# Second layer of a four-layer image network: one kept query projection and keys-first softmax attention without row maxima or transposes

## The chip, the cores and the metric

The kernel runs on one core of a Trainium2 chip. The metric is the device time of one execution in microseconds (us), as a median over runs. All runs that are compared in this document were fast: none was over 1.5% above the fastest of its kernel. A profile of one execution stands beside each kernel. Its engines are PE (TensorE matmuls), PEld (TensorE weight loads), DVE (VectorE), ACT (ScalarE), POOL (GpSimd) and SP (SyncE). PEclk is the share of full speed that TensorE's clock was granted.

## The reference

Four layers, each `x = x + layer(group_norm(x))`, run on two images of 512 channels and 64x64 pixels. The change concerns the second layer, an attention with 8 heads of 64 channels. Its 256 keys and values come from bilinear samples of the query image at places that the queries themselves choose:

```python
q = einsum('oc,bchw->bohw', w_q, x)
oi = q.reshape(b * g, inner // g, h, w)          # 8 offset groups
...                                              # offsets from every 4th pixel of oi
kv_feats = grid_sample_bilinear(oi, vgrid)       # 16 x 16 samples of q
k, v = split(einsum('oc,bchw->bohw', w_kv, kv_feats))
...
sim = einsum('bhid,bhjd->bhij', qh * 64 ** -0.5, kh)   # 4096 queries, 256 keys
out = einsum('bhij,bhjd->bhid', softmax(sim), vh)
return einsum('oc,bchw->bohw', w_out, out) + b_out
```

## The kernel before

Everything is float32. P = 128 partitions, C = 512 channels in KC = 4 chunks of 128 (two heads each), blocks of TB = 512 tokens (NB = 8 of them), NT = 4 token tiles in a block, NK = 256 keys. Two image buffers fill most of SBUF; the second (Y) lends its space to weights in this layer. The queries are projected twice: once with tokens on partitions for the sampling, and once per block for the attention.

```python
# sampling, for each of 32 token tiles t
for kc in range(KC):
    matmul(ps, X[:, kc, t * P:(t + 1) * P], wq[:, kc, :], ...)      # q, tokens first
vector.tensor_tensor(q, ps, row, ALU.add)
...                                       # wt = max(0,1-|dy|) max(0,1-|dx|), 128x2048
for g in range(NH):
    cc, lo = g // 2, (g % 2) * HD
    matmul(acc[lo:lo + HD, cc, :NK], q[:, g * HD:(g + 1) * HD], wt[:, g, :], ...)
# attention: for blk in range(NB), for cc in range(KC)
self.project(ps, wq[:, :, cc * P:(cc + 1) * P], X, blk)             # q again, channels first
scalar.activation(q, ps, AF.Identity, bias=bq[:, cc:cc + 1], scale=HD ** -0.5)
for h in range(2):
    self.scores(pS, q, keys[:, cc, :], h)        # tokens first: 4 matmuls of 256 columns
    vector.tensor_reduce(nm, pS, AX.X, ALU.max, negate=True)        # row maxima
    for t in range(NT):
        scalar.activation(prob[:, t, :], pS[:, t, :], AF.Exp, bias=nm[:, t:t + 1],
                          accum_out=sm[:, t:t + 1])
    vector.reciprocal(sm, sm)
    vector.tensor_tensor(prob, prob, bcast(sm, 2, NK), ALU.mult)
    self.weighted(psO, prob, vals[...], h, wp, pp)   # 8 transposes, 2 copies, 2 matmuls
scalar.copy(att[:, cc, :], psO)
# after the four chunks: self.add_projected(X, wo, att, blk, pp, bias)
```

## Time and profile before

| kernel before | value |
|---|---|
| time | 10124.43 us, median of 3 runs (10123.72 to 10126.53) |
| second layer, first image: sampling | 2259.6 to 2453.4 = 193.8 us |
| keys and values | to 2468.2 = 14.8 us |
| attention with output projection | to 3230.2 = 762 us |
| second image | the same stages about 5050 us later |

The page opens with the busy time of each engine, its share of the span and its number of instructions.

```profile
span 10124.4 us, 68201 instructions
PE 8632.9 (85%) x25390; PEld 4059.3 (40%) x25390; DVE 4276.9 (42%) x7503; ACT 2048.9 (20%) x4873; POOL 1093.5 (11%) x1190
```

Eighty-five per cent of PE says that PE matters, but not where there is slack; the prediction looks for that stage by stage.

### The profile page before, as it was taken

Reading aid. Unit: us, or ns where it says so; the run is one execution under the profiler, and the core shown is the slowest. Engines: PE = TensorE matmul, PEld = TensorE weight load, DVE = VectorE, ACT = ScalarE, POOL = GpSimd, SP = SyncE. Lnnn points to the kernel's source line nnn. Section 1 sums busy time; section 2 is a strip of 40 time slices with the busy share of each in tenths; the row PEclk is TensorE's granted clock in tenths of the full one; section 3 lists DMA queues with packets and bytes.
Section 4 is the critical chain, followed back from the end, with each engine's and each line's share of the span. In section 5 each row is a group of like instructions: output and inputs, shape, how many; then the busy total and the mean of one; then the engine's idle time right before and its main releaser. Section 6 shows DMA issues by size and latency. Waiting matters only on the chain. (4 is left out here: it accounts for less than half of the span.)

```text
span 10124.4 us, 68201 instructions
## 1 busy us (share of the span) xinstructions
PE 8632.9 (85%) x25390; PEld 4059.3 (40%) x25390; DVE 4276.9 (42%) x7503; ACT 2048.9 (20%) x4873; POOL 1093.5 (11%) x1190
## 2 busy tenths in 40 slices
PE   7989898988786699888889898989888876998887
PEld 3333333344333255544443333333443332555443
DVE  3444444425334922244434444444352359222343
ACT  1111111105222101222211111111142221022222
POOL 0222222200000000000002222222000000100000
PEclk9878888889887889977788887887898888899877
DMA  1000000000000000100000000000000000000000
GB/s 46 0 4 0 3 0 0 0 22 1 0 0 9 1 0 5 38 9 13 9 15 0 4 0 4 0 0 0 22 1 0 0 9 1 0 5 5 13 9 13
DMA packets 34324, 66.76 MB, mean 7 GB/s; under 512 B 2532, under 2 KB 15076, under 8 KB 32970
## 3 DMA queue, kind: packets, MB, share of 16 engines
q1 hardware_dynamic: 33994, 62.40, 1.8%
q8 instruction: 202, 3.31, 0.1%
q14 instruction: 128, 1.05, 0.0%
HBM read 45.62 MB, written 16.78 MB: 6 GB/s over the span
## 5 line engine op out<-in xcount | busy, mean ns | idle before, releaser
L122 PE MATMUL mm<-big,w 128*128 128x512 f32 x2560 | 1371.4, 682 | 0.0
L122 PEld LDWEIGHTS mm<-big,w 128*128 128x128 f32 x2560 | 532.6, 221 | 727.4 <-issue 639.9
L449 POOL TENSOR_TENSOR acc<-acc,prod 128x512 f32<-128x512 f32 x512 | 663.4, 1296 | 1441.3 <-DVE prod L444 1392.6
L442 PE MATMUL mm<-lt,taps 18*128 18x512 f32 x1152 | 761.2, 804 | 0.0
L166 PE MATMUL mm<-cst,prob 128*128 128x128 f32 x2048 | 429.7, 370 | 273.0 <-DVE prob L524 247.9
L388 PE MATMUL mm<-prod,cst 128*18 128x512 f32 x1152 | 648.5, 713 | 0.0
L169 DVE COPY pT<-mm 128x512 f32<-128x512 f32 x384 | 265.5, 691 | 787.4 <-PE mm L166 787.4
L166 PEld LDWEIGHTS mm<-cst,prob 128*128 128x128 f32 x2048 | 342.7, 194 | 511.3 <-issue 508.7
L154 PE MATMUL pS<-proj,big 64*128 64x256 f32 x2048 | 459.4, 444 | 98.5 <-ACT big L772 49.9
L444 DVE TENSOR_TENSOR prod<-vx,mm 128x512 f32<-128x512 f32 x512 | 351.9, 687 | 443.9 <-PE mm L442 356.6
L384 DVE TENSOR_TENSOR prod<-qs,kx 128x512 f32<-128x512 f32 x576 | 443.2, 800 | 195.6 <-PE mm L388 194.3
L713 PE MATMUL acc<-big,dg 128*128 128x512 f32 x768 | 369.0, 639 | 136.3 <-DVE big L681 71.4
L171 ACT COPY pT<-mm 128x512 f32<-128x512 f32 x384 | 224.8, 585 | 1000.8 <-PE mm L166 1000.8
L681 DVE TENSOR_TENSOR big<-big 128x3968 f32<-128x3968 f32 x96 | 410.4, 4286 | 21.2 <-PE acc L713 18.3
L442 PEld LDWEIGHTS mm<-lt,taps 18*128 18x128 f32 x1152 | 241.4, 232 | 424.9 <-issue 245.9
L154 PEld LDWEIGHTS pS<-proj,big 64*128 64x128 f32 x2048 | 307.1, 211 | 242.4 <-ACT big L772 103.7
L166 PE MATMUL mm<-cst,qf 128*128 128x128 f32 x1024 | 207.1, 354 | 219.0 <-DVE qf L884 219.0
L420 ACT ACTIVATE prob<-pS,nm 128x256 f32<-128x256 f32 x512 | 235.8, 473 | 630.9 <-DVE nm L415 625.7
L173 PE MATMUL psO<-pT,ctxm 128*64 128x512 f32 x512 | 334.2, 788 | 33.0 <-ACT pT L171 33.0
L173 PE MATMUL psO<-pT,vals 128*64 128x512 f32 x512 | 361.7, 800 | 0.0
L516 DVE TENSOR_REDUCE nm<-pS 128x4 f32<-128x1024 f32 x128 | 150.7, 1219 | 480.8 <-PE pS L154 480.8
L154 PE MATMUL pS<-proj,q 64*128 64x256 f32 x1024 | 280.2, 522 | 53.4 <-ACT q L863 53.4
(267 smaller groups left out, 11377.5 us busy)
## 6 DMA issues: line engine op xcount, KB each, us to landing
big<-in_x SPq DMA_DIRECT2D x8, 2048.0 KB, 8.3
out<-big SPq DMA_DIRECT2D x16, 1024.0 KB, 4.1
w<-in_W_kv SPq DMA_DIRECT2D x16, 256.0 KB, 3.8
big<-in_w_kv SPq DMA_DIRECT2D x2, 2048.0 KB, 7.8
w_sr<-in_W_sr SPq DMA_DIRECT2D x2, 1024.0 KB
w<-in_W_q SPq DMA_DIRECT2D x8, 256.0 KB, 3.0
w_proj<-in_W_proj SPq DMA_DIRECT2D x2, 1024.0 KB, 5.4
big<-in_w_out SPq DMA_DIRECT2D x2, 1024.0 KB
```

The source lines that it names most:

```text
L122: self.nc.tensor.matmul(ps, w[:, kc, :], X[:, kc, blk * TB:(blk + 1) * TB], start=(kc == 0), stop=(kc == KC - 1))
L154: self.nc.tensor.matmul(pS[:, t, :], q[lo:lo + HD, t * P:(t + 1) * P], keys[lo:lo + HD, :], start=True, stop=True)
L166: nc.tensor.transpose(ps[:, t * P:(t + 1) * P], prob[:, t, k2 * P:(k2 + 1) * P], self.ident)
L169: nc.vector.tensor_copy(pT, ps)
L173: nc.tensor.matmul(psO[h * HD:(h + 1) * HD, :], vals[:, k2, :], pTs[k2], start=(k2 == 0), stop=(k2 == 1))
L384: nc.vector.tensor_tensor(pr.rearrange("p (y x) -> p y x", x=W), qs.rearrange("p (y x) -> p y x", x=W), kx[:, dy:dy + 8, dx:dx + W], ALU.mult)
L388: nc.tensor.matmul(ps[:18, :], self.cst[:, C_TAP + 8 - k:C_TAP + 26 - k], pr, start=(k == 0), stop=(k == 8))
L442: nc.tensor.matmul(ps, taps[:, k, :], lt, start=True, stop=True)
L444: nc.vector.tensor_tensor(pr.rearrange("p (y x) -> p y x", x=W), vx[:, dy:dy + 8, dx:dx + W], ps.rearrange("p (y x) -> p y x", x=W), ALU.mult)
L449: nc.gpsimd.tensor_tensor(acc, acc, pr, ALU.add)
L681: nc.vector.tensor_tensor(o, a, b, ALU.max)
L713: nc.tensor.matmul(accs[b], dg, p2[:, b * TB:(b + 1) * TB], start=(j == 1), stop=(j == 6))
```

## The change

The intent is to project the queries once, keep them in the spare image buffer for the whole layer, and form the scores with keys on partitions. Exponentials of keys-first scores can go into the value product directly, so the transposes fall away. The sum over keys becomes a product with ones, and the division is done once on the small result. A row maximum is awkward in that form, so it is left out. A bound on |q| times |k| is computed instead; only if it exceeds 40 does the whole general program (the old code) run again at the end. For the given inputs the bound is under 9. The diff, cut to its core; the output projection of block b is now issued two steps late, and the scores of step i+1 are issued before the values of step i:

```diff
+        def query(blk):                                   # in sampling, a block ahead
+            for cc in range(KC):
+                self.project(ps, wq[:, :, cc * P:(cc + 1) * P], X, blk)
+                nc.scalar.activation(Y[:, cc, blk * TB:(blk + 1) * TB], ps, AF.Identity,
+                                     bias=bq[:, cc:cc + 1])
         for each token tile t:
-            4 matmuls of 512 columns (q, tokens first), DVE adds the row, DVE and 2 ACT passes for wt
+            nc.scalar.activation(wt, ycoord, AF.Abs, bias=yneg[:, t:t + 1])
+            nc.vector.tensor_scalar(wt, wt, -1.0, 0.0, ALU.add, ALU.min)
+            nc.vector.tensor_tensor(wt, wt, hatx, ALU.mult)
+            for cc in range(KC):
+                nc.tensor.transpose(ps[:, cc * P:(cc + 1) * P], Y[:, cc, t * P:(t + 1) * P], ident)
+            nc.scalar.copy(q, ps)
...
+    def product_bound(self, q, keys, sp, pp):             # after the values
+        nc.vector.tensor_reduce(top[:, :, 0], q, AX.X, ALU.max, apply_absolute_value=True)
+        nc.vector.tensor_reduce(top[:, :, 1], keys, AX.X, ALU.max, apply_absolute_value=True)
...
+    def exponentials(self, q, keys, wp, pp):
+        for j in range(2):                                # 128 keys each
+            pS = [pp.tile([P, TB], F32, name="mm") for _ in range(2)]
+            for h in range(2):
+                nc.tensor.matmul(pS[h], keys[h * HD:(h + 1) * HD, j * P:(j + 1) * P],
+                                 q[h * HD:(h + 1) * HD, :], start=True, stop=True)
+            for h in range(2):
+                nc.scalar.activation(prob[h][j], pS[h], AF.Exp)
+        for h in range(2):
+            nc.gpsimd.tensor_tensor(total[h], prob[h][0], prob[h][1], ALU.add)
+    def attended(self, out, made, vals, wp, ppo, ppd):
+        for j in range(2):
+            for h in range(2):
+                nc.tensor.matmul(psO[h * HD:(h + 1) * HD, :], vals[:, j, h * HD:(h + 1) * HD],
+                                 prob[h][j], start=(j == 0), stop=(j == 1))
+        for h in range(2):
+            nc.tensor.matmul(psD[h * HD:(h + 1) * HD, :], self.one[:, :HD], total[h], ...)
+        nc.vector.reciprocal(r, psD)
+        nc.vector.tensor_tensor(out, psO, r, ALU.mult)    # into Y, over the used queries
```

More of the change, by code (lines that the diff above doesn't have):

```diff
@@ L25 @@
 NK = 256
+LIMIT = 40.0
+RISKS = 16
 C_ID, C_GRP, C_MEAN, C_ONE, C_E2, C_TAP, C_Y, C_X, C_MH = (
@@ L50, in in_turn @@
         gens = [g for g in gens if next(g, gens) is not gens]
-class Net:
+class General:
+    risk = None
     def __init__(self, tc, cst, vec):
@@ L914, in softplus, with layer1, query_and_sample, at_most @@
         return out
+class Net(General):
+    def layer1(self, X, Y, d):
+        tc, nc, vec = self.tc, self.nc, self.vec
+        with tc.tile_pool(name="l1", bufs=1) as sp:
+            wq = sp.tile([P, KC, C], F32, name="wq1")
+            nc.sync.dma_start(wq, d["w_q1"].rearrange("(kc p) o -> p kc o", p=P))
+            wkv = sp.tile([P, KC, 2 * C], F32, name="wkv1")
+            nc.sync.dma_start(wkv, d["w_kv1"].rearrange("(kc p) o -> p kc o", p=P))
+            bq = sp.tile([P, KC], F32, name="bq1")
+            feats = sp.tile([P, KC, NK], F32, name="feats")
+            with tc.tile_pool(name="l1a", bufs=1) as wp, \
+                    tc.tile_pool(name="l1p", bufs=4, space=PSUM) as pp, \
+                    tc.tile_pool(name="l1k", bufs=1, space=PSUM) as ppk:
+                grid = wp.tile([P, 2, NK], F32, name="grid")
+                nc.sync.dma_start(grid, d["grid"])
+                nmean, rstd, _ = self.group_stats(X, sp, pp)
+                self.scale_rows(wq, rstd)
+                self.shift_bias(bq, wq, nmean, pp)
+                ycoord, hatx = self.sample_grid(X, wq, bq, grid, wp, pp)
+                self.query_and_sample(X, Y, wq, bq, ycoord, hatx, feats, wp, pp, ppk)
+            with tc.tile_pool(name="l1c", bufs=1) as late:
+                keys = late.tile([P, KC, NK], F32, name="keys")
+                vals = late.tile([P, 2, C], F32, name="vals")
+                with tc.tile_pool(name="l1q", bufs=4, space=PSUM) as pp:
+                    for oc in range(KC):
+                        ps = pp.tile([P, TB], F32, name="mm")
+                        for kc in range(KC):
+                            nc.tensor.matmul(ps[:, :NK], wkv[:, kc, oc * P:(oc + 1) * P],
+                                             feats[:, kc, :], start=(kc == 0), stop=(kc == KC - 1))
+                        nc.scalar.mul(keys[:, oc, :], ps[:, :NK], HD ** -0.5)
+                    for t in range(2):
+                        ps = pp.tile([P, TB], F32, name="mm")
+                        for kc in range(KC):
+                            nc.tensor.matmul(ps, feats[:, kc, t * P:(t + 1) * P], wkv[:, kc, C:],
+                                             start=(kc == 0), stop=(kc == KC - 1))
+                        nc.vector.tensor_copy(vals[:, t, :], ps)
+                    self.product_bound(Y, keys, sp, pp)
+                with tc.tile_pool(name="l1b", bufs=2) as wp, \
+                        tc.tile_pool(name="l1s", bufs=5, space=PSUM) as pp, \
+                        tc.tile_pool(name="l1o", bufs=2, space=PSUM) as ppo, \
+                        tc.tile_pool(name="l1d", bufs=1, space=PSUM) as ppd:
+                    wo = wp.tile([P, KC, C], F32, name="wo1", bufs=1)
+                    nc.sync.dma_start(wo, d["w_out1"].rearrange("(kc p) o -> p kc o", p=P))
+                    steps = [(blk, cc) for blk in range(NB) for cc in range(KC)]
+                    probs = {}
+                    for i in range(len(steps) + 2):
+                        if i < len(steps):
+                            blk, cc = steps[i]
+                            probs[i] = self.exponentials(Y[:, cc, blk * TB:(blk + 1) * TB],
+                                                         keys[:, cc, :], wp, pp)
+                        if 1 <= i <= len(steps):
+                            blk, cc = steps[i - 1]
+                            self.attended(Y[:, cc, blk * TB:(blk + 1) * TB], probs.pop(i - 1),
+                                          vals[:, :, cc * P:(cc + 1) * P], wp, ppo, ppd)
+                        if i >= 2 and steps[i - 2][1] == KC - 1:
+                            blk = steps[i - 2][0]
+                            self.add_projected(X, wo, Y[:, :, blk * TB:(blk + 1) * TB], blk, pp,
+                                               vec[:, V_BOUT:V_BOUT + KC])
+    def query_and_sample(self, X, Y, wq, bq, ycoord, hatx, feats, wp, pp, ppk):
+        nc = self.nc
+        acc = ppk.tile([P, KC, TB], F32, name="acc")
+        n_t = N // P
+        yneg = wp.tile([P, n_t], F32, name="yneg")
+        nc.vector.tensor_scalar(yneg, self.cst[:, C_Y:C_Y + n_t], -1.0, None, ALU.mult)
+        nc.vector.tensor_scalar(hatx, hatx, -1.0, None, ALU.mult)
+        def query(blk):
+            for cc in range(KC):
+                ps = pp.tile([P, TB], F32, name="mm")
+                self.project(ps, wq[:, :, cc * P:(cc + 1) * P], X, blk)
+                nc.scalar.activation(Y[:, cc, blk * TB:(blk + 1) * TB], ps, AF.Identity,
+                                     bias=bq[:, cc:cc + 1])
+        query(0)
+        for blk in range(NB):
+            if blk + 1 < NB:
+                query(blk + 1)
+            for t in range(blk * NT, (blk + 1) * NT):
+                wt = wp.tile([P, NH, NK], F32, name="wt", bufs=2)
+                nc.scalar.activation(wt, ycoord, AF.Abs, bias=yneg[:, t:t + 1])
+                nc.vector.tensor_scalar(wt, wt, -1.0, 0.0, ALU.add, ALU.min)
+                nc.vector.tensor_tensor(wt, wt, hatx, ALU.mult)
+                ps = pp.tile([P, TB], F32, name="mm")
+                for cc in range(KC):
+                    nc.tensor.transpose(ps[:, cc * P:(cc + 1) * P], Y[:, cc, t * P:(t + 1) * P],
+                                        self.ident)
+                q = wp.tile([P, C], F32, name="q_tok", bufs=2)
+                nc.scalar.copy(q, ps)
+                for g in range(NH):
+                    cc, lo = g // 2, (g % 2) * HD
+                    nc.tensor.matmul(acc[lo:lo + HD, cc, :NK], q[:, g * HD:(g + 1) * HD],
+                                     wt[:, g, :], start=(t == 0), stop=(t == n_t - 1))
+        nc.vector.tensor_copy(feats, acc[:, :, :NK])
+    def product_bound(self, q, keys, sp, pp):
+        nc = self.nc
+        top = sp.tile([P, KC, 2], F32, name="top_qk")
+        nc.vector.tensor_reduce(top[:, :, 0], q, AX.X, ALU.max, apply_absolute_value=True)
+        nc.vector.tensor_reduce(top[:, :, 1], keys, AX.X, ALU.max, apply_absolute_value=True)
+        nc.vector.tensor_tensor(top[:, :, 0], top[:, :, 0], top[:, :, 1], ALU.mult)
+        ps = pp.tile([P, TB], F32, name="mm")
+        nc.tensor.matmul(ps[:2, :KC], self.e2, top[:, :, 0], start=True, stop=True)
+        self.at_most(ps[:2, :KC])
+    def at_most(self, bounds):
+        nc = self.nc
+        n = bounds.shape[0]
+        nc.vector.tensor_reduce(self.risk[:n, self.risks:self.risks + 1], bounds, AX.X, ALU.max)
+        self.risks += 1
+    def exponentials(self, q, keys, wp, pp):
+        nc = self.nc
+        prob = [[wp.tile([P, TB], F32, name="prob", bufs=8) for _ in range(2)] for _ in range(2)]
+        for j in range(2):
[5 more added lines that the diff above has]
+                nc.scalar.activation(prob[h][j], pS[h], AF.Exp)
+        total = [wp.tile([P, TB], F32, name="total", bufs=4) for _ in range(2)]
+        for h in range(2):
+            nc.gpsimd.tensor_tensor(total[h], prob[h][0], prob[h][1], ALU.add)
+        return prob, total
+    def attended(self, out, made, vals, wp, ppo, ppd):
+        nc = self.nc
+        prob, total = made
+        psO = ppo.tile([P, TB], F32, name="psO")
+        for j in range(2):
+            for h in range(2):
+                nc.tensor.matmul(psO[h * HD:(h + 1) * HD, :], vals[:, j, h * HD:(h + 1) * HD],
+                                 prob[h][j], start=(j == 0), stop=(j == 1))
+        psD = ppd.tile([P, TB], F32, name="psD")
+        for h in range(2):
+            nc.tensor.matmul(psD[h * HD:(h + 1) * HD, :], self.one[:, :HD], total[h], start=True,
+                             stop=True)
+        r = wp.tile([P, TB], F32, name="recip")
+        nc.vector.reciprocal(r, psD)
+        nc.vector.tensor_tensor(out, psO, r, ALU.mult)
+    def risky(self, sp, limit):
+        nc = self.nc
+        with self.tc.tile_pool(name="risk", bufs=1, space=PSUM) as pp:
+            top = sp.tile([P, 1], F32, name="top_risk")
+            nc.vector.tensor_reduce(top, self.risk, AX.X, ALU.max)
+            ps = pp.tile([P, TB], F32, name="mm")
+            nc.tensor.transpose(ps[:1, :P], top, self.ident)
+            nc.vector.tensor_reduce(top[:1, :], ps[:1, :P], AX.X, ALU.max)
+        nc.vector.tensor_scalar(top[:1, :], top[:1, :], limit, None, ALU.is_gt)
+        whole = sp.tile([1, 1], I32, name="whole_risk")
+        nc.vector.tensor_copy(whole, top[:1, :])
+        return nc.values_load(whole[0:1, 0:1])
@@ L917, in tile_net @@
 @with_exitstack
-def tile_net(ctx: ExitStack, tc: tile.TileContext, d, out, layers=4, batches=2):
+def tile_net(ctx: ExitStack, tc: tile.TileContext, d, out, layers=4, batches=2, limit=LIMIT):
     nc = tc.nc
@@ L926, in tile_net, with whole_net @@
     nc.sync.dma_start(tokT, d["tok"])
-    big = [cp.tile([P, KC, N], F32, name=f"big{i}") for i in range(2)]
+    sp_scale = General(tc, cst, vec).softplus(cp)
     net = Net(tc, cst, vec)
-    sp_scale = net.softplus(cp)
+    net.risk, net.risks = cp.tile([P, RISKS], F32, name="risk"), 0
+    nc.vector.memset(net.risk, 0.0)
+    whole_net(tc, net, d, out, sp_scale, tokT, layers, batches)
+    with tc.If(net.risky(cp, limit) > 0):
+        whole_net(tc, General(tc, cst, vec), d, out, sp_scale, tokT, layers, batches)
+@with_exitstack
+def whole_net(ctx: ExitStack, tc: tile.TileContext, net, d, out, sp_scale, tokT, layers, batches):
+    nc = tc.nc
+    bp = ctx.enter_context(tc.tile_pool(name="images", bufs=1))
+    big = [bp.tile([P, KC, N], F32, name=f"big{i}") for i in range(2)]
     def load(X, b):
@@ L1011, in arrays_of, with build @@
     return {f"in_{k}": np.ascontiguousarray(v) for k, v in arrays.items()}
-def build(arrays, layers=4, batches=2):
+def build(arrays, layers=4, batches=2, limit=LIMIT):
     import concourse.bacc as bacc
@@ L1021, in build @@
     with tile.TileContext(nc) as tc:
-        tile_net(tc, d, out, layers=layers, batches=batches)
+        tile_net(tc, d, out, layers=layers, batches=batches, limit=limit)
     return nc
```

## The prediction

> **What bounds the kernel now.** I read the busy table first: PE is busy 85% of 10124 us, every other engine under half. Such an average mixes four layers, so I next found the stretches of the second layer from the first and last start of its tiles, and asked for the busy time per stretch. For the first image, weights and offsets are set up until about 2260 us, sampling runs to 2454, keys and values to 2468, attention and its output projection to 3230. The second image repeats this about 5050 us later. Columns: busy us and record count of PE, PEld, DVE, ACT, POOL, then the granted clock.
>
> ```profile
> 2265.00:2455.00 190.00, 170.85 (x757) 79.75 (x756) 130.20 (x94) 117.06 (x63) 0.00 (x0) 0.98 0.00 1
> 2475.00:3232.00 757.00, 607.06 (x1773) 280.32 (x1771) 245.12 (x310) 198.34 (x640) 0.22 (x2) 0.86 0.00 1
> ```
>
> Attention is the large piece: 757 us, of which PE idles 150. One of its 32 steps (a block of 512 tokens and a pair of heads) in order of time, from one query evacuation to the next:
>
> ```profile
> 2814.24 2.84 PE L122 MATMUL mm<-big,wq 128*128 128x512 f32 x6
> ...
> 2817.12 0.69 ACT L509 ACTIVATE q<-mm,bq 128x512 f32<-128x512 f32 x1 [2.19 <-PE mm L122]
> ...
> 2817.86 2.96 PE L154 MATMUL pS<-keys,q 64*128 64x256 f32 x16 [0.78 <-ACT q L509]
> 2819.89 2.35 DVE L516 TENSOR_REDUCE nm<-pS 128x4 f32<-128x1024 f32 x2 [7.91 <-PE pS L154]
> 2821.14 0.47 ACT L520 ACTIVATE prob<-pS,nm 128x256 f32<-128x256 f32 x1 [3.34 <-DVE nm L516]
> ...
> 2823.32 1.22 DVE L524 TENSOR_TENSOR prob<-prob,sm 128x1024 f32<-128x1024 f32 x1
> ...
> 2824.69 1.94 PE L166 MATMUL mm<-cst,prob 128*128 128x128 f32 x8 [3.87 <-DVE prob L524]
> 2824.94 0.18 DVE L523 RECIPROCAL sm<-sm 128x4 f32<-128x4 f32 x1 [0.39 <-ACT prob L520]
> 2825.15 1.23 DVE L524 TENSOR_TENSOR prob<-prob,sm 128x1024 f32<-128x1024 f32 x1
> 2825.81 0.59 ACT L171 COPY pT<-mm 128x512 f32<-128x512 f32 x1 [0.91 <-PE mm L166]
> ```
>
> The step repeats every 20.47 us (the row maxima start at 2799.42 and 2819.89). PE holds a serial chain: project the query, wait for its evacuation (0.78), scores, then wait 3.87 us for maxima, exponentials and scaling, then transposes with copies, then values. PE's own work is about 13 us of the 20.5; the rest is this chain, since little of the next step is started early.
>
> **What a record costs.** A float32 matmul shows as two records. In the sampling stretch:
>
> ```profile
> 2259.59 8.75 PE L594 MATMUL mm<-wq,big 128*128 128x512 f32 x20
> 2272.54 1.95 PE L606 MATMUL acc<-wt,q_tok 128*64 128x256 f32 x16
> ```
>
> The first gives (8.75-0.2)/20 = 0.4275 us per record of 512 columns (0.2 is the modelled tail of the last). A record of 256 columns should then take 0.214, but the second line, whose outputs alternate between the two halves of the output partitions, gives (1.95-0.2)/16 = 0.109: two at a time. The scores above, 16 records of 256 on half the rows, would take 3.42 alone and start over 2.6 us; cutting the stretch into quarter microseconds shows the middle ones starting 0.107 apart, where the two heads' records meet. So both halves of rows and halves of columns can run in pairs. A transpose costs (1.94-0.2)/8 = 0.217. Going between half-array and whole-array work costs about 0.17 us (the 16 records above start at 2272.54 and hold 1.71 us of work; the next kind starts at 2274.41).
>
> **What the Trainium skill says.** "TensorE: Matmul & The Clock Gate", Part 3 (Packing small matmuls — row/col tiling), says small matmuls on different row or column groups run concurrently; this trace agrees with the 0.109 above. "TensorEngine Tiling (Array Packing)", Key Properties, says changing the tiling mode drains the engine; the 0.17 us agrees. "VectorE: DVE Perf Modes", the fixed hardware budget, says reciprocal is an iterative divide "with a repeat count of 8". The trace has only 128x4 ones, 178 ns, where two-input operations of that shape take 150 to 164. Over a base of 150 that leaves about 6 to 7 ns per element: an estimate of 3.4 us for 128x512, and 8 cycles at the page's 0.96 GHz would give 4.4. "SBUF — State Buffer", Who interferes with whom, says a VectorE operation with at most one SBUF input outside the two-port modes does not contend with GpSimd; the new VectorE work in attention reads PSUM plus at most one SBUF tensor, so I expect GpSimd's new additions at the 1.26 us that its 128x512 addition in layer 0 takes. No stretch of this trace tests it in this layer.
>
> **The change, part by part, per image.**
>
> *Sampling.* The token-first projection is replaced by the query projection, kept in the spare image buffer for attention, plus 4 transposes per token tile. PE: 128 matmuls x 2 x 0.4275 = 109.4, 128 transposes x 0.217 = 27.8, 512 records x 0.107 = 54.8, together 192. The instruction order has about six changes of array mode per block of four tiles: 48 x 0.17 = 8. ACT loses one 1.9 us pass of 128x2048 per tile and gains a 0.59 copy and a 0.69 evacuation; DVE per tile is 1.28 + 2.29 = 3.6. Both are below PE's 6.3 per tile. But the new bound takes a maximum over all queries, 128x16384 elements; from 1219 ns for 1024 that is 17 us on DVE, and the order puts it after the 26th of 32 tiles, where PE has no more projections to fill with. The last six tiles then go at DVE's pace: I charge 15 us. 215 in all, against 193.8 (first projection 2259.6 to last product 2453.4): +21.
>
> *Keys, values.* The same 14 us of matmuls; key maxima (1.2 us) and the product run beside the value matmuls. 0.
>
> *Attention.* Removed per step: query projection (3.4), 16 transposes (3.5), all row maxima, scaling, transposed copies. Left for PE: scores 8 records of 512 in alternating heads, 8 x 0.4275/2 = 1.71; values the same, 1.71; the sums by a ones matmul, 4 records, 0.86; two mode changes, 0.35. Sum 4.63. The other engines per step: ACT four exponentials of 128x512, about 0.55 each (1.81 between starts for 2048 gives 0.43 + 0.11), 2.2; POOL two additions, 2.6; DVE reciprocal 3.4 + product 0.69 = 4.1. The order is scores of step i+1, values and sums of step i, so exponentials and additions (about 5.5 us from the start of scores) are in time for sums needed some 8 us later. The sums have one PSUM buffer: the next sums wait for the reciprocal, 3.7 us after the last with hand-overs, while PE has 1.71 + 1.71 + 0.35 = 3.8 to do between. That just fits; I take 4.9 per step for it. The output projection stays: 32 x 0.4275 = 13.7, and 0.2. A block is 4 x 4.9 + 13.9 = 33.5, eight are 268; filling and emptying the pipeline 9: 277, against 762 (2468.2 to 3230.2): -485.
>
> *Boundary.* The next layer's statistics (32 x 0.63 us on DVE) ran after 3217, only at the end; the new order puts 14 of them between earlier blocks. I take -5.
>
> *End.* The bound is compared early in layer 3; at the end each engine loads a flag and branches over the general program, about +6 once. I worked out the bound from the reference's inputs: under 9 against the limit 40, so the general program is skipped.
>
> Sum: 2 x (21 + 0 - 485 - 5) + 6 = -932: 9192. Hand-overs are more often missed than invented, so I set 9205.
>
> **Rivals.**
> 1. *VectorE's reciprocal becomes the bound.* For: the sums have one buffer and PE's slack is 0.1 us; the skill's count of 8. Against: the 13.9 us projection after each four steps lets it catch up, and 178 ns for four elements hardly allows 8 cycles each. At 4.4 us three steps in four stall by some 1 us: 2 x 8 x 3 x 1 = +50, 9250.
> 2. *Heads do not pair in scores or values.* For: only 256-column records are seen paired, and the two heads wait on different buffers. Against: the 16-record line, and the alternating order in the instruction list. If the scores alone don't pair, 64 x 1.71 = +110, 9310; if nothing does, +275, 9475.
> 3. *Sampling takes more back.* Transposes, ACT's copies and PE in turn may chain per tile (0.4 + 0.6 + 0.4 us); if half of the 64 tiles expose 1 us more, +32. If instead DVE's maximum is hidden, -30.
> 4. *The gain is hidden because another engine bounds the layer.* Nothing speaks for it: DVE per block is 4 x 4.1 + 4 x 0.73 + 1.3 = 20.6 us beside PE's 32.5.
>
> **Range and chances.** The terms that can move are the step (4.65 to 5.7, so -16 to +51), sampling (-30 to +35), the end (0 to +15) and partial pairing. They mostly add time, hence 9140 to 9310. Even no pairing at all leaves over 6%. Faster by over 2%: 0.985; within 2%: 0.01; slower: 0.005, the general program running after all.
>
> **What would show it.** Right: attention steps 4.7 to 5 us apart, PE over 90% busy there; score records of 512 columns starting about 0.21 apart on average; a reciprocal of 3 to 4.4 us; one 17 us maximum late in sampling with PE waiting after it; 21 us longer sampling; other layers unmoved. Wrong: score records 0.43 apart; PE waiting for the reciprocal in most steps; sampling over 235 us; a tail of tens of us after the last output; or a second run of layer 0.

## The result, and the profile after

| | before | after |
|---|---|---|
| median, us | 10124.08 (10117.26 to 10126.53, 4 runs) | 9170.66 (9156.89 to 9172.28, 4 runs) |
| sampling, first image | 193.8 | 215.2 |
| keys and values | 14.8 | 16.2 |
| attention | 762.0 | 260.5 |
| idle PE until the next layer's first matmul | 14.2 | 12.9 |

The ratio is 0.9055, 95% interval 0.9042 to 0.9068. Ratios here are the mean time of one kernel's fast runs over the mean of the other's fast runs of the same rounds, so not quite the ratio of the quoted medians. The head of the page after:

```profile
span 9170.2 us, 63972 instructions
PE 7959.0 (87%) x23843; PEld 3715.6 (41%) x23843; DVE 4117.4 (45%) x7064; ACT 1742.4 (19%) x3917; POOL 1252.4 (14%) x1318
```

PE lost 674 us of busy time, while the span lost 954. The other 280 us were idle PE. Busy time per stretch, for sampling and then attention (columns as in the prediction: length, busy us and records of PE, PEld, DVE, ACT, POOL, then the granted clock):

```profile
2265.00:2455.00 190.00, 174.78 (x802) 88.82 (x802) 114.95 (x58) 92.94 (x90) 0.00 (x0) 0.96 0.00 1
2495.00:2752.00 257.00, 257.00 (x887) 92.36 (x885) 164.03 (x115) 65.32 (x128) 79.80 (x64) 1.00 0.03 9
```

In attention PE is never idle, and its clock is 1.00, where it was 0.86 before. One step in order of time:

```profile
2536.79 1.99 PE L1053 MATMUL mm<-big,keys 64*128 64x512 f32 x8
2536.93 3.36 DVE L1076 RECIPROCAL recip<-psD 128x512 f32<-128x512 f32 x1 [3.93 <-PE psD L1073]
...
2538.01 2.07 ACT L1056 ACTIVATE prob<-mm 128x512 f32<-128x512 f32 x4 [2.58 <-PE mm L1053]
...
2538.70 1.94 PE L1069 MATMUL psO<-prob,vals 128*64 128x512 f32 x8
...
2539.66 2.50 POOL L1059 TENSOR_TENSOR total<-prob 128x512 f32<-128x512 f32 x2 [2.16 <-ACT prob L1056]
2540.32 0.69 DVE L1077 TENSOR_TENSOR big<-psO,recip 128x512 f32<-128x512 f32 x1
...
2540.47 1.04 PE L1073 MATMUL psD<-total,cst 128*64 128x512 f32 x4
...
2541.45 1.13 PE L1053 MATMUL mm<-big,keys 64*128 64x512 f32 x4
2541.57 3.36 DVE L1076 RECIPROCAL recip<-psD 128x512 f32<-128x512 f32 x1 [0.56 <-PE psD L1073]
```

The scores start at 2536.79 and again at 2541.45, so a step takes 4.66 here (4.64 to 4.66 in the steady part). No PE line has an idle time in brackets: the chain of waits is gone. DVE has only 0.56 us to spare between its product and the next reciprocal. A block of four steps with its output projection takes 32.54 us (2532.14 to 2564.68), and eight of them are the whole stage.

The price of it stands near the end of sampling:

```profile
2432.16 17.22 DVE L1031 TENSOR_REDUCE top_qk<-big 128x4 f32<-128x16384 f32 x1 [3.90 <-ACT big L1003]
...
2451.56 4.49 DVE L1014 TENSOR_TENSOR wt<-wt,hatx 128x2048 f32<-128x2048 f32 x2
2453.90 2.40 PE L1023 MATMUL acc<-wt,q_tok 128*64 128x256 f32 x10 [13.69 <-DVE wt L1014]
```

The maximum over all queries holds DVE for 17.22 us. The sampling weights that stand behind it come late, and PE waits 13.69 us for them.

Added up over both images: a later start (+4.4 us: the first statistics begin at 15.0 instead of 10.5), 2 x (20.9 sampling, the mean of 21.4 and 20.4, + 1.5 keys - 501.5 attention - 1.3 boundary), and 2.2 more after the last output. That is -954.2, as measured between the two profiled spans. The unedited stretches moved too, by -2.4 us before the first sampling, +3.1 between the images and -0.7 after the second, but these cancel.

### The profile page after: what moved, and what is told of

Its sections match the earlier page's. It is cut to its first block, busy times and chain, and to the rows that moved or that the text cites. A ratio compares the mean times of both kernels' runs of the same rounds, so it can differ in the third digit from the quotient of the medians.

```text
span 9170.2 us, 63972 instructions
## 1 busy us (share of the span) xinstructions
PE 7959.0 (87%) x23843; PEld 3715.6 (41%) x23843; DVE 4117.4 (45%) x7064; ACT 1742.4 (19%) x3917; POOL 1252.4 (14%) x1318
## 5 line engine op out<-in xcount | busy, mean ns | idle before, releaser
L391 DVE TENSOR_TENSOR prod<-qs,kx 128x512 f32<-128x512 f32 x576 | 443.4, 801 | 195.1 <-PE mm L395 193.8
L176 DVE COPY pT<-mm 128x512 f32<-128x512 f32 x256 | 177.0, 692 | 492.9 <-PE mm L173 492.9
L161 PE MATMUL pS<-kp,qs 64*128 64x256 f32 x1024 | 316.0, 424 | 0.0
L173 PEld LDWEIGHTS mm<-cst,qf 128*128 128x128 f32 x1024 | 161.8, 185 | 375.5 <-issue 317.6
L148 PE MATMUL mm<-cst,hn_re 128*128 128x128 f32 x528 | 118.0, 363 | 225.2 <-DVE hn_re L145 200.8
L395 PEld LDWEIGHTS mm<-prod,cst 128*18 128x18 f32 x1152 | 113.7, 110 | 464.8 <-issue 377.2
L803 POOL TENSOR_TENSOR sq<-q 128x512 f32<-128x512 f32 x64 | 66.4, 1038 | 1710.8 <-ACT q L870 1710.8
```

The lines of the kernel that those rows point to most:

```text
L161: self.nc.tensor.matmul(pS[:, t, :], q[lo:lo + HD, t * P:(t + 1) * P], keys[lo:lo + HD, :], start=True, stop=True)
L173: nc.tensor.transpose(ps[:, t * P:(t + 1) * P], prob[:, t, k2 * P:(k2 + 1) * P], self.ident)
L391: nc.vector.tensor_tensor(pr.rearrange("p (y x) -> p y x", x=W), qs.rearrange("p (y x) -> p y x", x=W), kx[:, dy:dy + 8, dx:dx + W], ALU.mult)
L395: nc.tensor.matmul(ps[:18, :], self.cst[:, C_TAP + 8 - k:C_TAP + 26 - k], pr, start=(k == 0), stop=(k == 8))
```

## The experiments

Twelve kernels ran, in three groups, each group on one chip beside runs of the kernel before. Their medians of the kernel before were 10127.5, 10125.6 and 10123.4 us. All changed kernels gave the right result except where said otherwise. "Per image" numbers are of the first image.

### The changed kernel again

The kernel after, unedited, for comparison within its group.

> The changed kernel unedited, beside the next three on one chip: 9170 us, within 10. It gives the yardstick for differences of a few tenths of a per cent.

Measured: 9167.21 us (9163.91 to 9175.23), ratio 0.9053, with stages of 215.2, 16.2 and 260.5 us. The kernel after is reproduced.

### What the bound's maximum costs

First, the maximum reads 128 of the 4096 tokens. The output is right for these inputs, but the bound is then unsafe; this is a measurement and no proposal.

```diff
-        nc.vector.tensor_reduce(top[:, :, 0], q, AX.X, ALU.max, ...)
+        nc.vector.tensor_reduce(top[:, :, 0], q[:, :, :P], AX.X, ALU.max, ...)
```

> The maximum over the queries looks at 128 tokens of the 4096 only, so the bound is no longer safe (the output stays right for these inputs). My theory: the 17.2 us maximum stands late in sampling, where PE has no projections left, and PE waits 13.7 us for the weights behind it; removed, each image's sampling shortens by 13 to 16 us, the whole by some 28, to about 9142. Rival: the end of sampling is paced by VectorE anyway and by the buffers of the weights, so most of the 17 us comes back as another wait: under 10 us in all.

Measured: 9140.25 us (ratio 0.9026), sampling 201.5 in place of 215.2. Two times 13.7 is 27.4, and the whole fell by 27.0. So the maximum costs 13.7 us per image.

Then the full bound is kept, but its maximum is taken block by block, right after each block's queries are made:

```diff
         def query(blk):
             ...
+            nc.vector.tensor_reduce(tops[:, :, blk], Y[:, :, blk * TB:(blk + 1) * TB], AX.X,
+                                    ALU.max, apply_absolute_value=True)
```

> The same maximum in eight pieces of 128x2048, each after its block's queries, so the work is kept and only its place changes. Theory: VectorE has 25 us per block and needs 14.3 + 2.2, so the pieces are hidden and nearly all of the gain of the shortened maximum comes: about -26 us, 9144. Rival: a piece delays the weights of its block and PE waits eight times for 1 to 2 us: no gain.

Measured: 9135.03 us (ratio 0.902), sampling 201.9. The same work on DVE, cut in eight, is hidden. One piece of it and its neighbours:

```profile
2275.64 2.28 DVE L1006 TENSOR_REDUCE tops<-big 128x4 f32<-128x2048 f32 x1
2287.99 2.29 DVE L1006 TENSOR_REDUCE tops<-big 128x4 f32<-128x2048 f32 x1 [10.07 <-ACT big L1004]
```

Eight times 2.29 is 18.3 us, even a little more than the single 17.22. DVE was idle 10.07 us before the second piece. The cost was in the place of the instruction, not in its size.

Last, the same, with the softplus set-up moved behind the first image's load, so that the load does not wait for it:

```diff
-    sp_scale = General(tc, cst, vec).softplus(cp)      # before the image buffers' pool
...
     load(big[0], 0)
+    sp_scale = net.softplus(bp)
```

> The spread maximum, and the images' buffers allocated before the softplus of the temperature instead of after it. Theory: the first image's load now need not wait for softplus's scratch space, which its buffer overlays, so the first statistics start at 10.5 us as before the change and not at 15.0: another -4.4 us, 9140. Rival: the load ends when it did and nothing changes.

Measured: 9126.83 us (9123.27 to 9132.59), ratio 0.9011, with the first statistics at 11.3. It beats both kernels: 40 us less than the kernel after in the same group. Sampling gives 13.8 and 12.9 us of that and the start 3.4. Of the rest, 8.6 us lie in the last layer of the second image, whose code is unedited; I could not settle why.

### What the reciprocal costs

A second, unused reciprocal of the same sums is added:

```diff
         nc.vector.reciprocal(r, psD)
+        nc.vector.reciprocal(again, psD)
```

> The reciprocal of the sums is taken a second time, into a buffer that nobody reads: 6.7 us in place of 3.36 per step. Theory: at 3.36 it is just hidden (PE starts the next sums 0.2 us after it ends); doubled, VectorE has 4 x 7.4 + 4.3 = 34 us per block against PE's 32.5 and bounds the attention, and the instruction order, which is decided with the durations in view, puts the sums later: a block of 34 to 37 us, +25 to +70 in all. Rival: the reciprocal already sets the step, so doubling it adds 3.36 to each step: +215.

Measured: 9272.10 us (ratio 0.9155), attention 304.6, so +44 per image, and the idle PE behind it is 19.6 us in place of 12.9. That is more than I had expected. PE waits now:

```profile
2545.93 3.29 DVE L1078 RECIPROCAL again<-psD 128x512 f32<-128x512 f32 x1
...
2549.37 1.08 PE L1073 MATMUL psD<-total,cst 128*64 128x512 f32 x4 [1.91 <-DVE again L1078]
```

The sums have one PSUM buffer, and they wait 1.91 us for its last reader. The direction was clear, but I under-estimated the size: between two projections the first reciprocals now start 7.83 us apart (2542.66 and 2550.49), of which DVE waits 0.72 for sums that could not start before the second reciprocal had ended.

The opposite: the reciprocal is replaced by a copy of the same size. Its output is wrong, which doesn't matter for the time.

```diff
-        nc.vector.reciprocal(r, psD)
+        nc.vector.tensor_copy(r, psD)
```

> Wrong on purpose: a copy in place of the reciprocal, 0.7 us in place of 3.36, so the output is wrong. Theory: PE bounds the step, nothing comes of it but the last step of each image, where the output projection waits for the reciprocal (about 1 us): 0 to -4, 9167. Rival: the single sums buffer makes the reciprocal the pace: step down by several tenths of a us, -20 or more.

Measured: attention 259.9, only 0.6 us per image less. The copy takes 0.69 us in place of 3.36, and the step is still 4.64. So the reciprocal as it stands is hidden within the stage. Behind the stage it is not: PE's idle time until the next layer's first matmul falls from 12.9 to 8.9 us, as DVE comes sooner to that layer's statistics. The whole took 9149.07 us, some 18 to 20 less than the kernel after. These two differences make 9 us of that over both images; another 8.9 lie in the last layer of the second image (1526.6 us in place of 1535.5), which is unedited and not explained.

### Without the look-ahead

Scores, values and sums of the same step follow each other; the output projection follows its block at once.

```diff
-                        if i < len(steps): probs[i] = self.exponentials(step i)
-                        if 1 <= i <= len(steps): self.attended(step i - 1)
+                        probs[i] = self.exponentials(step i)
+                        self.attended(step i)
```

> Each step's values and sums right after its own scores, in place of one step later; the same instructions. Theory: PE now waits for exponentials and for the two additions on GpSimd, whose second ends 5.4 us after the scores start: a step of about 6.4 us in place of 4.64, and each block's projection waits some 1.8 us for the last reciprocal: 64 x 1.8 + 16 x 1.8 = +145, about 9315. Rival: the order on PE is mended by the queue or the scheduler and nothing changes.

Measured: 9280.80 us (ratio 0.9166), attention 317.1, +56 per image, with a step of 6.42 us (scores at 2537.28 and 2543.70 us). The loss was a little smaller than expected. It is real: without the look-ahead, PE waits in each step for the exponentials and for POOL's additions.

### Does the order of the heads matter?

My first theory of the pairs was that heads must alternate in the instruction list. So here both matmuls of a head follow each other, in scores and in values:

```diff
-        for j in range(2):
-            for h in range(2):
+        for h in range(2):
+            for j in range(2):
```

> The same instructions, but each head's two key halves one after the other, in scores and in values, in place of the heads in turn. Theory (pairs): two matmuls on one half of the array cannot overlap, only the middle two of the four do, so scores take 3 x 0.855 = 2.57 us in place of 1.71, and values with sums 3.42 in place of 2.57: a step of 6.3 us in place of 4.64, 64 x 1.7 = +109 us, about 9280. Rival: the gain comes from the smaller count of instructions alone and the order does not matter: unchanged, 9170. A second rival, no overlap at all in this order, would give +165.

Measured: 9169.00 us (ratio 0.9056), attention 261.5. The theory fell.

```profile
2532.49 1.99 PE L1053 MATMUL mm<-big,keys 64*128 64x512 f32 x8
2534.41 1.95 PE L1069 MATMUL psO<-prob,vals 128*64 128x512 f32 x8
2536.18 1.03 PE L1073 MATMUL psD<-total,cst 128*64 128x512 f32 x4
2537.14 2.00 PE L1053 MATMUL mm<-big,keys 64*128 64x512 f32 x8
```

Eight records of 512 columns still fit in 1.92 us, though the list has head 0, head 0, head 1, head 1. Two explanations were left. Either a matmul on half the array runs its own two records side by side, and the other head does not matter. Or a matmul of head 1 starts past the second one of head 0, which is still waiting. Two more kernels tell these apart.

In the first, the heads are kept apart by work of another kind. Per step: scores of head 0, values of head 0 (of the step before), scores of head 1, values of head 1, then the sums of both.

```diff
-  scores h0,h1 (j0), scores h0,h1 (j1) | values h0,h1 (j0), values h0,h1 (j1) | sums h0, h1
+  scores h0 (j0, j1) | values h0 (j0, j1) | scores h1 (j0, j1) | values h1 (j0, j1) | sums h0, h1
```

> The two heads' matmuls are kept apart by other work in between: per step scores of head 0, values of head 0, scores of head 1, values of head 1, then the sums. Correct output. If two matmuls of one head on the same half of the array cannot run side by side, and only the two heads' can, all 16 records of scores and values take 0.4275 each: 3.42 + 3.42 + 0.86 (sums, still paired) + 4 changes of array mode of 0.17 = 8.4 us per step against 4.64, 64 x 3.75 = +240, about 9410 (9350 to 9450). If the two records of one matmul on half the array run side by side by themselves, the step is 1.71 + 1.71 + 0.86 + 0.68 = 5.0 and the whole 9190 to 9210.

Measured: 9400.64 us (9394.93 to 9404.13, ratio 0.9285), and the reciprocals are 8.41 us apart. Both numbers are those of the pairs between heads.

```profile
2570.88 1.93 PE L1070 MATMUL psO<-prob,vals 128*64 128x512 f32 x4
2572.74 1.98 PE L1060 MATMUL mm<-big,keys 64*128 64x512 f32 x4
2574.65 0.64 PE L1070 MATMUL psO<-prob,vals 128*64 128x512 f32 x1
2574.66 0.64 PE L1077 MATMUL psD<-total,cst 128*64 128x512 f32 x1
...
2575.56 1.02 PE L1070 MATMUL psO<-prob,vals 128*64 128x512 f32 x2
2576.42 1.02 PE L1077 MATMUL psD<-total,cst 128*64 128x512 f32 x2
```

The first two lines are one head alone: four records in 1.9 us, where the kernel after has eight. The next ones show more than I had asked for. The list has two value matmuls of head 1, then the sum of head 0, then the sum of head 1. The sum of head 0 (other half of the array) starts at 2574.66 beside the first value matmul of 2574.65, while the second value matmul waits until 2575.56. It has started past one waiting matmul. (Building the kernels of this section again shows the order of the text in TensorE's instruction list, so it was not the scheduler that moved the sum ahead.)

In the second kernel, the scores are cut into 256 columns, so that a head has four matmuls in a row:

```diff
-  matmul(pS[j], keys of h, j, q of h)                          # 512 columns, h inside j
+  for j in range(2): for s in range(2):                        # inside h
+      matmul(pS[j][:, half s], keys of h, j, q of h [:, half s])   # 256 columns
```

> The scores are cut into halves of 256 columns: four matmuls of head 0, then four of head 1, as the kernel before had them. Correct output. With two matmuls per head in a row the order cost nothing (the run with the heads in order). If a matmul can start on the other half of the array past one waiting matmul but not past two or three, only the last one or two of head 0 meet the first of head 1: about 0.86 + 0.86 + 0.86 = 2.58 us of scores per step in place of 1.71, 64 x 0.87 = +56, about 9225 (9205 to 9240). If the order never matters, however long a head's row is, nothing changes: 9165 to 9180.

Measured: 9234.84 us (9225.09 to 9236.85, ratio 0.9119), step 5.62.

```profile
2579.53 2.96 PE L1055 MATMUL mm<-big,keys 64*128 64x256 f32 x16
2582.43 1.94 PE L1071 MATMUL psO<-prob,vals 128*64 128x512 f32 x8
```

The scores take 2.90 us to the start of the values, against 1.92 in the kernel with two in a row; the same columns are processed. If a matmul can start past one waiting matmul, six matmul times of 0.43 are needed for the eight (0.43 x 6 = 2.6). Past none it would be seven (3.0), past two five (2.1). With the 0.2 us of change that the 1.92 holds over its 1.71, the measured 2.90 leaves 2.7. So one is the number that fits. The single records in the trace show it directly: head 0's third matmul starts at 2580.50 and head 1's first at 2580.51, while head 0's fourth waits until 2580.93. They show the last 0.1 us too: each head's first record is 0.32 us from its second, the others 0.216, and here the two heads pay that one after the other. It also fits the 2.96 us of the 16-record score line that the prediction shows of the kernel before.

### The two halves of the change

Here the new sampling with kept queries runs with the old attention loop. Then the row maxima are taken out of that loop as well.

```diff
 # old attention, first kernel
-    self.project(ps, wq..., X, blk); scalar.activation(q, ps, ...)
+    q = Y[:, cc, blk * TB:(blk + 1) * TB]
 # second kernel, in addition
-    vector.tensor_reduce(nm, pS, AX.X, ALU.max, negate=True)
-    scalar.activation(prob[:, t, :], pS[:, t, :], AF.Exp, bias=nm[:, t:t + 1], ...)
+    scalar.activation(prob[:, t, :], pS[:, t, :], AF.Exp, ...)
```

> Only the first half of the change: the kept query projection and the new sampling, with the old attention loop (row maxima, scaling by the sums, transposes) reading its queries from the spare image buffer. It splits the gain of some 955 us into what the kept queries give and what the keys-first form gives. Removed against before per step: the query projection (3.4 us of PE) and the wait for its evacuation (0.8). If the step stays a serial chain, it falls from 20.5 to about 16.2 us, 32 x 16.2 = 518 and eight projections of 13.9, 630 per image, the whole 9910. If the ready queries let the next step's scores run in the waits of this one, the step tends to PE's own work plus a little, about 12.5, 511 per image, the whole about 9670. I expect the second, 9500 to 9800, since nothing but two PSUM buffers of scores holds the next scores back. If the keys-first form did nothing, it would be at 9170.

> As the run with the old attention on kept queries, but without the row maxima: the exponentials read the scores straight away (the result stays correct, since the scores are small). It tells whether the maxima's 2.35 us of VectorE per head were on the path. If the steps overlap and PE is the bound, taking the maxima away gives little (0 to 60 us of the whole); if the chain is serial, it gives 2 to 3.5 us in each of 64 steps, 130 to 220 us.

Measured: 9709.02 us (9697.36 to 9726.66, ratio 0.9596) and 9542.28 us (9539.16 to 9555.31, ratio 0.943). So the kept queries bring about 415 us, the missing maxima 167 more, and the keys-first form the other 375 or so, down to the 9167 that the kernel after took in its own group. The first lay near the expected 9670. The second lay in the range that I had given to a serial chain, although the steps do overlap in the first. What it means stands in the two kernels' attention stretches (PE busy us and records, then PEld, DVE, ACT, POOL, and the clock):

```profile
2490.00:3017.00 527.00, 496.18 (x1527) 239.96 (x1524) 248.76 (x311) 179.36 (x610) 0.09 (x2) 0.85 0.01 4
```

```profile
2495.00:2942.00 447.00, 435.81 (x1522) 212.55 (x1521) 172.14 (x246) 155.66 (x610) 0.00 (x0) 0.97 0.02 5
```

PE has practically the same records in both, but is busy 60 us longer in the first, at a clock of 0.85. Of the 80 us between the stretches, idle time explains only (527.0 - 496.2) - (447.0 - 435.8) = 20. The rest is the same matmuls at a slower clock. One such place in the first kernel, the wait and then the clock (length, PE busy us and records, clock):

```profile
2585.86 3.11 PE L161 MATMUL pS<-keys,big 64*128 64x256 f32 x8 [1.60 <-ACT prob L985]
```

```profile
2583.16:2586.57 3.41, 1.81 (x6) 1.00 0.00 0
2586.57:2600.23 13.66, 13.66 (x32) 0.50 0.00 0
2600.23:2613.88 13.65, 13.65 (x33) 1.00 0.00 0
```

The wait before the clock falls is only 1.60 us, and PE then works 13.66 us without a pause at half clock. PE waits 13 times for exponentials in this stretch, 25.1 us in all, and twelve of these waits are of 1.60 or 1.98 us; eleven of the twelve are followed by 6.8 to 17.1 us at half clock. With the maxima left out, such waits come to 7.6 us. Why the half clock lasts so long here stays open.

## Why the prediction was right

**What bounds the kernel: right, with one thing overlooked.** The serial chain was there, and the kernel after has none of it. But I had read the clock of 0.86 in the attention stretch and made nothing of it. The step that the prediction shows, asked again for PE alone (length, PE busy us and records, clock):

```profile
2817.80:2820.80 3.00, 2.94 (x16) 1.00 0.00 0
2820.80:2824.60 3.80, 0.02 (x1) 0.90 0.00 0
2825.00:2830.00 5.00, 5.00 (x15) 0.50 0.01 3
2832.00:2841.00 9.00, 9.00 (x21) 1.00 0.00 0
```

Scores at full clock, the 3.87 us wait, then at least five us of transposes and value products at half clock, then full clock again. In one-microsecond slices the clock falls about 3.0 us into the wait and comes back about 6 us after PE has resumed; in other steps it falls 1.5 to 3.6 us into the same wait. The Trainium skill, "TensorE: Matmul & The Clock Gate", Part 1 (The HAM clock gate), says that the array drops to half clock after an idle window of about 3.4 us and returns after a window of sustained work. This step agrees with that roughly; the kernel with the old attention on kept queries does not, with its waits of 1.60 us. So the wait of 3.87 us costs a second time: some 6 us of work per step ran at half speed, about 3 us lost. Over 64 steps that makes some 190 us of the time before, an estimate from these lines. The prediction put 20.5 - 13 = 7.5 us of a step down to the chain; PE idled only 150 / 32 = 4.7 of them, and the half clock is most of the rest. The pair of kernels with and without maxima shows directly what a slower clock costs. The predicted step was still right, because its record times came from stretches at full clock and the new step has no wait that would lower it; the measured clock there is 1.00.

**What a record costs: one term mis-sized.** 0.4275 for a record, half for a pair, and 0.17 for a change of array mode stood the test. The 0.217 for a transpose did not: its eight records lay in the half-clock stretch. In the sampling of the kernel after, at full clock:

```profile
2360.70 1.36 PE L1017 MATMUL mm<-cst,big 128*128 128x128 f32 x11
```

That is (1.36 - 0.2)/11 = 0.105.

**Sampling +21: right sum, two wrong terms.** With 0.105 the 128 transposes take 13.5 us, not 27.8. PE's own work is then about 186 us with mode changes, and 29 us are left for the end of the stage, where I had charged 15. The profile has 21.7 us of PE's waits for DVE's weights and 1.2 for ACT's copies in the whole stage, and the half clock after the 13.69 us wait. The maximum itself costs 13.7 of it, shown by two kernels; the other 15 stayed in them (201.5). With the maximum spread, PE still waits 8.5 us for the last tiles' weights, and the clock is 0.78 in the last 21.5 us, which I had not charged apart. The two errors of about 14 cancelled by chance.

**Keys 0, boundary -5.** Measured were +1.5 and -1.3. The statistics do run between earlier blocks, as predicted, but many of them need the last block, and DVE is busy with them until the end as before.

**Attention -485: -501.5.** The step was booked at 4.9 although its own sum was 4.63; it is 4.64. The allowance for hand-overs was not needed. "Filling and emptying" was booked at 9 us; eight blocks of 32.54 are 260.3 of the 260.5 measured, so it is 0.2: the keys' and values' matmuls and the output projections fill both ends. The estimated reciprocal of 3.4 us is 3.36, and POOL's additions take 1.27 us each beside DVE's work, against the 1.26 taken from layer 0.

**End +6.** It is +2.2. In its place there is a later start, +4.4, which I had not foreseen: the image buffer now lies over the scratch space of the softplus, so the first load is issued at 6.86 us instead of 2.12. Issuing it first gave back 3.4.

**The rivals.** VectorE as the bound: it is not, but it is near; 2.67 us less changes 0.6 us in the stage and 4 behind it, and 3.29 more cost 44 and 7 us per image. No pairs: refuted by the times, and the kernel with the heads kept apart shows the price, 8.41 us per step. Sampling: the chains per tile did not appear (1.2 us of waits for copies). Why the order in the list was not needed was the part of my picture that failed, and the two kernels above settled it. The predicted 9205 stands against 9170.66: the sum was 9192, and I moved it up by 13 for missed hand-overs, which there were none of.

What stays open: why unedited stretches of the last layer differ by up to 9 us between kernels, and what sets the length of the half clock in the old attention on kept queries.

## What to carry to other kernels

A wait of PE can be paid twice, because the work after it may run at half clock: here after 3.87 us in each step of the kernel before, and after 1.60 us in another. Look at the clock of short stretches before taking a duration from them, and before judging what a wait is worth. An instruction of 17 us that nobody needs yet can still hold back the small ones behind it in the same queue; cut it into pieces that are issued where the engine has time. In these kernels half-array matmuls of two heads ran side by side as long as at most one waiting matmul stood between them in the list.

## What the Trainium skill lacked or had wrong

- "TensorE: Matmul & The Clock Gate", Part 3 (Packing small matmuls — row/col tiling), says of matmuls "strict FIFO, no reordering". Here a sum on the free half of the array started at 2574.66 us, while a value matmul that stands before it in the list waited until 2575.56. Past how many waiting matmuls this goes, no page says; here it is one (2.90 us for the scores in halves, 1.92 for those with two per head).
- The same page, Part 1, puts the half clock after an idle window of about 3.4 us and the return after about 3.4 us of sustained work. In the old attention on kept queries the clock fell after a wait of 1.60 us, in a window of 3.41 us in which PE was busy 1.81, and PE then worked 13.66 us without a pause before it came back (6.8 to 17.1 us after other such waits).
- "VectorE: DVE Perf Modes" names a repeat count of 8 for the reciprocal but no duration. A float32 reciprocal of 128x512 from PSUM took 3358 ns, a copy of the same tile 0.69 us: 5.2 ns more per element, about 5 cycles of the page's 0.96 GHz and not 8.
